# Layer 0 of a four-layer cross-attention stack: values summed by head, spread over the array by class, with one output matmul a tile, in place of values folded with the output weights

## The chip, the cores and the metric

One core of one Trainium2 chip runs the whole kernel in one launch. The metric is the device time in microseconds (us) of one execution. A profile of one execution gives the time of every instruction on TensorE (PE), VectorE (DVE), ScalarE (ACT), GpSimd (POOL) and the DMA queues that SyncE (SP) issues. All data are float32 but for the masks (bfloat16). A float32 matmul shows as two records (a weight load and a matmul each twice), so 8 matmuls are 16 records.

## What is computed

Four attention layers follow each other on 8 sequences of 256 positions and 128 features, with a context of 64 positions and 64 features. The change is in layer 0, cut here to what matters:

```python
q = (x @ Wq.T)            # B=8, L=256, 16 heads of 8 features
k = (ctx @ Wk.T) + pos    # M=64 context positions
v = (ctx @ Wv.T)
attn = softmax(q @ k.T * 8 ** -0.5)            # per head, over the 64 positions
attn_out = attn @ v                            # 16 heads of 8 features: 128
memory_output = attn_out @ Wo.T
gate = sigmoid(silu(concat(x, mean(ctx)) @ gate_w1.T + b1) @ gate_w2.T + b2)
enhanced = layernorm(x + gate * memory_output)
x = where(entropy(softmax(x @ ent_w)) > 1, enhanced, x)
```

Layer 1 is an attention with one head, layer 2 six blocks of self-attention (masked, 16 heads of 64), cross-attention and feed-forward, layer 3 an attention whose softmax runs over the positions of the sequence. These are the same before and after.

## The kernel before

The work stands in a plan. `at(tick, phase, fn)` enters a step; at the end (lines 1251 to 1261) the steps are written out tick by tick and, within a tick, by phase, and each engine takes its instructions in exactly that order. The engines wait for each other by semaphores alone. PSUM is a pool of four tiles of two banks each (line 37): every product takes the next free one, and its first matmul waits until the last reader of the tile before it there is done. SBUF tiles rotate within a tag in the same way.

Layer 0 handles sequence b in ticks from T = 2b on (`plan_l0`, lines 662 to 740), in two tiles of 128 queries. Tile number n (0 to 15) is thus handled in ticks n to n + 3, and several tiles are in flight at once. The steps of one tile (`plan_weights_64`, lines 314 to 399):

- `scores`, tick n, phase 1: 16 matmuls (L328) into two banks. Partition class a (32 partitions each) holds the heads 4a to 4a+3, the columns hold query block, head of the class and context position.
- `lower`, phase 2: ScalarE copies the scores to SBUF (L357), VectorE takes the maximum of each head (L359), which starts when the copy has ended, and GpSimd subtracts it (L360).
- `exps`, phase 8: ScalarE takes the exponential in place (L366).
- `divide`, tick n + 1, phase 2.4: VectorE sums and takes the reciprocal (L370, L371), GpSimd multiplies (L372).
- `turn`, tick n + 2, phase 2.5: VectorE turns 32x32 blocks (L380), so that the partitions hold the class and the context position.
- `sums`, tick n + 3, phase 3: 8 matmuls of 128x128 by 128 (L388) add up weights times folded values into the output of 128 queries by 128 features, and `take` (L687 on VectorE) applies the gate and adds the residual.

Beside these a sequence has, in even ticks, `queries` (L667, evacuated at L671, phase 3.3 of tick T - 2), `spread_keys` (GpSimd, L675), `make_values` (phase 3.2 of tick T + 2: 16 matmuls at L303, one copy of 128x1024 on ScalarE at L309), `moments` (phase 6 of T + 4: VectorE L262/L263 and four small steps on GpSimd, L265 to L696), in odd ticks `normal` (phase 2.95 of T + 5: ScalarE, L701 and L706) and `scaled` (phase 4.8: two transposes L713, evacuated at L715), and in even ticks `mix` (phase 4.7 of T + 6: two transposes L721, taken by L724). Layer 1 (`plan_l1`) follows for each sequence from tick 2b + 7 on, at phases 4.2 to 4.5: L749 and L780 are its transposes, L757, L761 and L789 its matmuls, L766, L778 and L794 its steps on VectorE, L751, L772 and L782 those on ScalarE. From tick 11 on the first projections of layer 2 (L861, L867, L880, L808 to L843) stand in the same ticks; its first scores (L898) come in tick 17.

The fold: since attn_out @ Wo.T is linear, the value weights and output weights of each head can be multiplied beforehand. `spread_outputs` (L523, GpSimd) spreads the output weights by head, `turn_values` (L530, L533) turns the value weights, and `fold_l0` (L545, four matmuls of 512 columns, and four copies on ScalarE, L552) makes WVO, 128 features for each head. `values_of` (lines 295 to 312) then multiplies the context with it. These steps stand in ticks -1, 1 and 2, among the steps that compute the gates (`gate_inputs` L490, `gate_hidden` L501 and L502, which takes turns between ScalarE and VectorE, `gates` L508), the logits (L447, after the selectors of L444) and the masks (L624, stored to DRAM by L631 and fetched later).

Two pairs of large tiles, `room` (line 85), hold the small weights of the start; the tag "eTc" that two of them come from is taken again by layer 2's weights from tick 17 on.

Of the kernel before, what the change touches and what calls it, by code (L numbers as in the profile page):

```python
# [16 lines left out]
P = 128  # L17
# [10 lines left out]
def tile_xattn_stack(ctx: ExitStack, tc: tile.TileContext, io, out: bass.AP):  # L28
# [22 lines left out]
    def tp_tile():  # L51
        return one_bank("tp")

    def mm_tile():
        return one_bank("mm")
# [134 lines left out]
        nc.vector.tensor_copy(hmask8[rows], hmask[rows, 8 * r : 8 * r + 8])  # L190


    W = {}

    def load_sa(l):
# [83 lines left out]
    def at(tick, phase, fn):  # L279
        plan.setdefault(tick, []).append((phase, fn))  # L280
# [33 lines left out]
    def plan_weights_64(tick, qt, qT, keys, values, mask, take):  # L314

        tl = {}

        def scores():  # L320
            sc = two_banks("sc").rearrange("p (q x) -> p q x", q=4)
            if mask is None:
                for i in range(4):
                    for a in range(4):
                        q = (i + 2 * (a // 2)) % 4
                        rows = slice(64 * (a // 2), 64 * (a // 2) + 64)
                        qb = 4 * qt + q
                        nc.tensor.matmul(  # L328
                            sc[32 * a : 32 * a + 32, q, :],
                            lhsT=qT()[rows, qb * 32 : (qb + 1) * 32],  # L330
                            rhs=keys()[rows, 4 * (a % 2) : 4 * (a % 2) + 4, :].rearrange(
                                "p h k -> p (h k)"
                            ),
                            start=True, stop=True,
                        )
                tl["sc"] = sc.rearrange("p q x -> p (q x)")
                return
            for q in range(4):
                qb = 4 * qt + q
                for a in range(4):  # L340
                    nc.tensor.matmul(  # L341
                        sc[32 * a : 32 * a + 32, q, :],
                        lhsT=qT()[:, qb * 32 : (qb + 1) * 32],
                        rhs=keys()[:, a].rearrange("p h k -> p (h k)"),
                        start=True, stop=False,
                    )
                for a in range(4):
                    nc.tensor.matmul(
                        sc[32 * a : 32 * a + 32, q, :], lhsT=ones0, rhs=mask,
                        start=False, stop=True,  # L350
                    )
            tl["sc"] = sc.rearrange("p q x -> p (q x)")

        def lower():
            sc = tl.pop("sc")
            e = big("e", shape=(P, 16, M))
            nc.scalar.copy(e.rearrange("p h k -> p (h k)"), sc)  # L357
            m = sm([P, 16], "m16")
            nc.vector.tensor_reduce(m, sc.rearrange("p (h k) -> p h k", k=M), AX.X, ALU.max)  # L359
            nc.gpsimd.tensor_tensor(  # L360
                e, e, m.unsqueeze(2).to_broadcast([P, 16, M]), ALU.subtract
            )
            tl["e"] = e

        def exps():
            nc.scalar.activation(tl["e"], tl["e"], AF.Exp)  # L366

        def divide():
            r = sm([P, 16], "r16")
            nc.vector.tensor_reduce(r, tl["e"], AX.X, ALU.add)  # L370
            nc.vector.reciprocal(r, r)  # L371
            nc.gpsimd.tensor_tensor(  # L372
                tl["e"], tl["e"], r.unsqueeze(2).to_broadcast([P, 16, M]), ALU.mult
            )

        def turn():
            e = tl.pop("e").rearrange("p (q h) (k x) -> p (h k) q x", q=4, x=32)
            eT = big("k" if mask is None else "o", shape=(P, 8, 4, 32))
            for i in range(2):
                nc.vector.transpose(eT[:, 4 * i : 4 * i + 4], e[:, 4 * i : 4 * i + 4])  # L380
            tl["eT"] = eT

        def sums():
            ps = mm_tile()
            eT, vw = tl.pop("eT"), values()
            for s in range(8):
                g, r, k = s // 4, s // 2 % 2, s % 2
                nc.tensor.matmul(  # L388
                    ps[:, :D], lhsT=eT[:, s].rearrange("p q x -> p (q x)"),
                    rhs=vw[:, r, k, g, :], start=(s == 0), stop=(s == 7),  # L390
                )
            take(ps)

        at(tick, 1, scores)
        at(tick, 2, lower)
        at(tick, 8, exps)
        at(tick + 1, 2.4, divide)
        at(tick + 2, 2.5, turn)
        at(tick + 3, 3.0, sums)


    S0 = {}
# [115 lines left out]
        nc.vector.tensor_copy(flag, ps[:, :B])  # L518
        nc.vector.tensor_scalar(nflag, flag, -1.0, 1.0, ALU.mult, ALU.add)

    def spread_outputs():
        S0["wobd"] = place("first", H * D).rearrange("p (h d) -> p h d", h=H)
        nc.gpsimd.tensor_tensor(  # L523
            S0["wobd"], w0o.unsqueeze(1).to_broadcast([P, H, D]),
            hmask.unsqueeze(2).to_broadcast([P, H, D]), ALU.mult,
        )

    def turn_values():
        tps = tp_tile()
        nc.tensor.transpose(tps[:, :DM], w0v, ident[:DM, :DM])  # L530
        wv2 = S0["wv2"] = place("second", P)
        for r in range(2):
            nc.scalar.copy(wv2[:, r * DM : (r + 1) * DM], tps[:, :DM])  # L533

    def fold_l0():


        wobd, wv2 = S0["wobd"], S0["wv2"]
        S0["WVO"] = sb([P, HC, D], "WVO", 1, heap)
        wvo = S0["WVO"].rearrange("p (g a) d -> p a g d", g=2)  # L540
        for half in range(2):
            ps = two_banks("mm")
            for i in range(2):
                a = 2 * half + i
                nc.tensor.matmul(  # L545
                    ps[:, i * 512 : (i + 1) * 512], lhsT=wv2,
                    rhs=wobd[:, 4 * a : 4 * a + 4].rearrange("p h d -> p (h d)"),
                    start=True, stop=True,
                )
            for r in range(2):  # L550
                rows = slice(r * DM, (r + 1) * DM)
                nc.scalar.copy(  # L552
                    wvo[rows, 2 * half : 2 * half + 2],
                    ps[rows].rearrange("p (a g r d) -> p a g r d", a=2, g=2, r=2)[:, :, :, r, :],
                )

    def fold_l1():

# [77 lines left out]
    def plan_start():  # L636
        at(-4, 0, lambda: turn_x(0))
        at(-4, 1, keys_l0)
        at(-4, 2, pool_context)
        at(-1, 0, spread_outputs)  # L640
        for c in range(1, 4):
            at(0, 3.1 + 0.1 * c, lambda c=c: turn_x(c))
        at(0, 3.6, gate_context)
        at(1, 3.0, gate_inputs)
        at(1, 3.1, gate_hidden)
        at(1, 3.2, turn_values)
        for i in range(4):
            at(1, 8.5, lambda i=i: mask(i))
        at(1, 8.6, store_masks)
        at(2, 3.1, fold_l0)  # L650
        at(2, 3.4, gates)
        at(2, 3.6, logits)
        at(3, 4, entropy)
# [8 lines left out]
    def plan_l0(b, T):  # L662
# [15 lines left out]
            )  # L678

        def make_values():  # L680
            st["VW"] = values_of(b, S0["WVO"])

        def add(qt, ps):
            if qt == 0:
# [57 lines left out]
    def plan_l1(b, T):  # L742
# [34 lines left out]
        def turn():  # L777
            nc.vector.reciprocal(st["r"], st["r"])  # L778
            tps = tp_tile()
            nc.tensor.transpose(tps[:, :P], st.pop("e"), ident)  # L780
            st["eT"] = sb([P, P], "o0")
            nc.scalar.copy(st["eT"], tps[:, :P])  # L782

        def values():
# [534 lines left out]
```

## Time and profile before

| what | us |
|---|---|
| median of 3 runs | 2443.6 (2442.93 to 2445.48) |
| the profiled execution | 2442.87 |
| its span, from the first to the last instruction | 2441.1 |
| PE busy, share of the span | 2349.7, 96% |
| DVE busy | 1839.3, 75% |
| ACT busy | 1718.1, 70% |
| POOL busy | 1450.2, 59% |
| PE busy from 0 to 44 us (the start, ticks 0 to 2) | 33.33 of 44 |
| PE busy from 44 to 145 us (ticks 3 to 16) | 93.28 of 101 |
| PE busy from 145 to 172 us (ticks 17 to 19) | 22.39 of 27 |
| PE busy from 172 us to the end | 2200.70 of 2269 |

Busy time of PE counts from the start of a matmul to its modelled end, so a PE that is busy is not PE at its peak. In the page's slices each digit is the busy share of a fortieth of the span (61 us) in tenths. A row of the timeline or of the groups is: start, length, engine, line, operation, output<-inputs, the form, how many, and in brackets the idle time before it with what ended it. For matmuls the form begins with the part of the array that is used: 128*32 is 128 rows and 32 columns. The chain of waits lists start, length and what: it follows the work that ended last back through what released it; cut to a window it begins with the last work of that window. A row of a table by windows has the stretch, its length, the busy time (and number) on PE, PE's weight loads, DVE, ACT and POOL, then the granted TensorE clock as a share of full speed, the DMA share and GB/s.

### The profile page before, as it was taken

How to read it: one execution, taken by the hardware profiler on the slowest of the kernel's cores; microseconds unless marked ns; L12 is line 12 of the kernel's file. 1: busy time of each engine (PE TensorE's matmuls, PEld its weight loads, DVE VectorE, ACT ScalarE, POOL GpSimd, SP SyncE). 2: the span in 40 equal slices, each digit the busy share in tenths (PEclk: the TensorE clock that was granted, in tenths of full speed). 3: DMA queues.
4: the chain of work that ended last, by engine and by line, in shares of the span. 5: the costliest groups of instructions: out<-in, count | busy, mean ns of one | idle time of the engine just before them, and what ended most of it. 6: DMA issues, size and time to landing. Idle time of an engine off the chain costs nothing.

```text
span 2441.1 us, 99984 instructions
## 1 busy us (share of the span) xinstructions
PE 2349.7 (96%) x42411; PEld 1742.3 (71%) x42411; DVE 1839.3 (75%) x5988; ACT 1718.1 (70%) x4528; POOL 1450.2 (59%) x2483
## 2 busy tenths in 40 slices
PE   8999999999999999999999999999999999999986
PEld 4667777777777677777777777777777777777764
DVE  5778887677887667887767887667888667888664
ACT  5577777677777667777667777667777667778642
POOL 4845557754556755556855556755556765555763
PEclk9999999999999999999999999999999999999998
DMA  6000022000022001022001022001012000010000
GB/s 177 2 11 14 23 75 57 2 12 21 20 72 64 2 3 30 20 72 64 2 3 30 20 63 64 11 3 30 20 55 72 12 2 26 24 53 5 2 3 16
DMA packets 102833, 76.88 MB, mean 31 GB/s; under 512 B 8113, under 2 KB 96881, under 8 KB 102386
## 3 DMA queue, kind: packets, MB, share of 16 engines
q1 hardware_dynamic: 101794, 70.16, 10.4%
q8 instruction: 334, 5.47, 0.9%
q14 instruction: 113, 0.93, 0.1%
q10 hardware_dynamic: 592, 0.33, 0.1%
HBM read 62.07 MB, written 8.39 MB: 29 GB/s over the span
## 4 chain that ended last, share of the span: by engine, by line
PE 77%; DVE 8%; ACT 7%; POOL 5%; issue 2%; DMA 0%; SPq 0%; POOLq 0%; DVEq 0%; ACTq 0%
PE mm L861 14%; PE sc L898 14%; PE mm L953 13%; PE mm L971 7%; PE mm L880 7%; PE mm L388 5%; PE sc L341 4%; PE mm L1120 3%; PE mm L1137 2%; DVE m L359 2%; ACT e L357 2%; POOL e L360 2%; PE mm L1079 2%; PE tp L841 1%; PE mm L303 1%
## 5 line engine op out<-in xcount | busy, mean ns | idle before, releaser
L927 POOL TENSOR_SCALAR e<-e,rs 128x256 f32<-128x256 f32 x1536 | 703.0, 478 | 673.3 <-DVE rs L925 664.0
L917 ACT ACTIVATE e<-e,mn 128x256 f32<-128x256 f32 x1536 | 758.2, 495 | 133.8 <-DVE mn L912 129.5
L912 DVE CUSTOM_DVE_ANT_0 e<-sc,nm 128x256 f32<-128x256 f32 x1536 | 542.4, 419 | 107.7 <-PE sc L898 106.2
L937 DVE STREAM_TRANSPOSE eTc<-e 128x512 f32<-128x512 f32 x768 | 517.3, 695 | 62.5 <-POOL e L927 61.2
L898 PE MATMUL sc<-k,q 64*32 64x256 f32 x12288 | 377.7, 380 | 1.9 <-ACT v L286 1.0
L953 PE MATMUL mm<-eTc,v 32*64 32x256 f32 x12288 | 363.9, 377 | 5.7 <-ACT AT L1054 3.3
L953 PEld LDWEIGHTS mm<-eTc,v 32*64 32x64 f32 x12288 | 277.3, 131 | 88.7 <-issue 22.7
L359 DVE TENSOR_REDUCE m<-sc 128x16 f32<-128x1024 f32 x112 | 136.7, 1221 | 269.2 <-ACT e L357 269.2
L360 POOL TENSOR_TENSOR e<-e,m 128x1024 f32<-128x1024 f32 x112 | 213.1, 1902 | 209.8 <-DVE m L359 209.8
L898 PEld LDWEIGHTS sc<-k,q 64*32 64x32 f32 x12288 | 221.3, 106 | 122.2 <-issue 48.9
L917 ACT ACTIVATION_READ_ACCUMULATOR e<-e,mn 128x1 f32 x1536 | 287.1, 187 | 0.0
L341 PE MATMUL sc<-q,tT 128*32 128x256 f32 x3072 | 222.0, 388 | 3.0 <-DVE t L1104 2.3
L372 POOL TENSOR_TENSOR e<-e,r 128x1024 f32<-128x1024 f32 x112 | 213.0, 1902 | 2.9 <-DVE r L371 2.9
L388 PE MATMUL mm<-v,o 128*128 128x128 f32 x1536 | 202.2, 287 | 0.0
L388 PEld LDWEIGHTS mm<-v,o 128*128 128x128 f32 x1536 | 188.9, 201 | 16.1 <-issue 8.7
L861 PE MATMUL mm<-tT,w_sk 128*128 128x256 f32 x768 | 189.1, 389 | 0.0
L971 PEld LDWEIGHTS mm<-w_sow,o 128*128 128x128 f32 x1536 | 175.1, 192 | 17.0 <-issue 12.3
L880 PE MATMUL mm<-w_sv,tT 128*32 128x256 f32 x3072 | 185.7, 382 | 0.0
L286 ACT COPY v<-mm 128x1024 f32<-128x1024 f32 x96 | 97.2, 1012 | 124.3 <-PE mm L880 123.7
L971 PE MATMUL mm<-w_sow,o 128*128 128x128 f32 x1536 | 183.6, 278 | 0.8 <-ACT WVO L1052 0.8
L861 PE MATMUL mm<-tT,w_sq 128*128 128x256 f32 x768 | 173.6, 379 | 0.0
L861 PEld LDWEIGHTS mm<-tT,w_sk 128*128 128x128 f32 x768 | 138.1, 190 | 44.1 <-issue 29.2
(212 smaller groups left out, 3544.5 us busy)
## 6 DMA issues: line engine op xcount, KB each, us to landing
nm<-mask_d SPq DMA_DIRECT2D x192, 128.0 KB
wd<-o SPq DMA_DIRECT2D x48, 128.0 KB
w_sk<-in_L_sa_kv_dram SPq DMA_DIRECT2D x6, 512.0 KB
w_sv<-in_L_sa_kv_dram SPq DMA_DIRECT2D x24, 128.0 KB
w_sq<-in_L_sa_q_dram SPq DMA_DIRECT2D x6, 512.0 KB
w_sow<-in_L_sa_ow_dram SPq DMA_DIRECT2D x6, 512.0 KB
w_ckv<-in_L_ca_kv_dram SPq DMA_DIRECT2D x12, 256.0 KB
w_cq<-in_L_ca_q_dram SPq DMA_DIRECT2D x6, 512.0 KB
```

The source lines that it names most:

```text
L341: nc.tensor.matmul(sc[32 * a : 32 * a + 32, q, :], lhsT=qT()[:, qb * 32 : (qb + 1) * 32], rhs=keys()[:, a].rearrange("p h k -> p (h k)"), ...
L360: nc.gpsimd.tensor_tensor(e, e, m.unsqueeze(2).to_broadcast([P, 16, M]), ALU.subtract)
L388: nc.tensor.matmul(ps[:, :D], lhsT=eT[:, s].rearrange("p q x -> p (q x)"), rhs=vw[:, r, k, g, :], start=(s == 0), stop=(s == 7),)
L861: nc.tensor.matmul(ps[:, i * S : (i + 1) * S], lhsT=w[:, c * P : (c + 1) * P], rhs=st["tT"], start=True, stop=True,)
L880: nc.tensor.matmul(ps[32 * a : 32 * a + 32, i, :], lhsT=st["tT"][:, kb * 32 : (kb + 1) * 32], rhs=sv[:, a].rearrange("p g x -> p (g x)"), ...
L898: nc.tensor.matmul(sc[32 * a : 32 * a + 32, r, j, :], lhsT=st["q"][g][rows, a, qb * 32 : (qb + 1) * 32], rhs=st["k"][g][rows, a, :], start ...
L912: nc.vector.tensor_tensor_reduce(e[:, i, :], sc4[:, i, :], st["nm"][:, 2 * jj + i % 2, :], -1.0, 3.0 * BIG, ALU.add, ALU.min, mn[:, i : i ...
L917: nc.scalar.activation(e[:, i, :], e[:, i, :], AF.Exp, scale=-1.0, bias=mn[:, i : i + 1], accum_out=rs[:, i : i + 1],)
L927: nc.gpsimd.tensor_scalar(e[:, i, :], e[:, i, :], rs[:, i : i + 1], 1.0, ALU.mult, ALU.mult)
L937: nc.vector.transpose(eT[:, r, :, 2 * jj : 2 * jj + 2, :], e[:, 2 * r : 2 * r + 2, :].rearrange("p j (k x) -> p k j x", x=32),)
L953: nc.tensor.matmul(ops[a // 2][r * HD : (r + 1) * HD, a % 2, :S], lhsT=st["v"][kb // 4][rows, kb % 4, (2 * g + r) * HD : (2 * g + r + 1) * ...
L971: nc.tensor.matmul(st["ps"][:, j * D : (j + 1) * D], lhsT=st["oT"][c // 4][:, c % 4, j * P : (j + 1) * P], rhs=sow[:, c, :], start=(c == 0 ...
```

## The change

Layer 0 no longer folds the output weights into the values. The values of a sequence are 8 features for each head: 8 matmuls of 64x32 weights by 32 columns, and one multiply on VectorE spreads them by class, with a mask `cmask` that leaves in partition class a only the 8 columns of the head that belongs to it (the array of 128 rows thus holds four heads at a time, and each sums only its own class). The sums of a tile are 8 matmuls of 128x32 weights by 128 queries, four column groups of the array in turn, two in each sum; they give the attention output with features on partitions. ScalarE copies it to SBUF (oT), and one matmul with the output weights, whose rows are put in the same order of features by `turn_outputs`, gives what `take` needs, at phase 4.6 of the same tick. In layer 0 the exponentials move from phase 8 of tick n to phase 2.05 of tick n + 1, behind the copy of the next tile's scores. `spread_outputs`, `turn_values` and `fold_l0` go. The tag "o0", which layer 1's L782 uses too, has three tiles in place of two. Layer 2's cross-attention shares `plan_weights_64` and keeps its steps.

```diff
@@ -188,6 +188,18 @@
     for r in range(2):
         rows = slice(64 * r, 64 * r + 64)
         nc.vector.tensor_copy(hmask8[rows], hmask[rows, 8 * r : 8 * r + 8])
+
+
+    cmask = const.tile([P, 4], F32, tag="cmask", name="cmask")
+    nc.gpsimd.memset(cmask, 1.0)
+    nc.gpsimd.affine_select(
+        out=cmask, in_=cmask, compare_op=ALU.is_ge, fill=0.0, base=0,
+        pattern=[[-32, 4]], channel_multiplier=1,
+    )
+    nc.gpsimd.affine_select(
+        out=cmask, in_=cmask, compare_op=ALU.is_ge, fill=0.0, base=31,
+        pattern=[[32, 4]], channel_multiplier=-1,
+    )
 
 
     W = {}
@@ -380,6 +392,26 @@
                 nc.vector.transpose(eT[:, 4 * i : 4 * i + 4], e[:, 4 * i : 4 * i + 4])
             tl["eT"] = eT
 
+        def sums_by_head():
+            ps = mm_tile()
+            eT, vw = tl.pop("eT"), values()
+            for k in range(2):
+                for j in range(4):
+                    nc.tensor.matmul(
+                        ps[32 * j : 32 * j + 32, :P], lhsT=vw[:, 4 * k + j, :],
+                        rhs=eT[:, 2 * j + k].rearrange("p q x -> p (q x)"),
+                        start=(k == 0), stop=(k == 1),
+                    )
+            tl["oT"] = sb([P, P], "o0", 3)
+            nc.scalar.copy(tl["oT"], ps[:, :P])
+
+        def outputs():
+            ps = mm_tile()
+            nc.tensor.matmul(
+                ps[:, :D], lhsT=tl.pop("oT"), rhs=S0["wo"], start=True, stop=True
+            )
+            take(ps)
+
         def sums():
             ps = mm_tile()
             eT, vw = tl.pop("eT"), values()
@@ -393,10 +425,15 @@
 
         at(tick, 1, scores)
         at(tick, 2, lower)
-        at(tick, 8, exps)
         at(tick + 1, 2.4, divide)
         at(tick + 2, 2.5, turn)
-        at(tick + 3, 3.0, sums)
+        if mask is None:
+            at(tick + 1, 2.05, exps)
+            at(tick + 3, 3.0, sums_by_head)
+            at(tick + 3, 4.6, outputs)
+        else:
+            at(tick, 8, exps)
+            at(tick + 3, 3.0, sums)
 
 
     S0 = {}
@@ -518,41 +555,17 @@
         nc.vector.tensor_copy(flag, ps[:, :B])
         nc.vector.tensor_scalar(nflag, flag, -1.0, 1.0, ALU.mult, ALU.add)
 
-    def spread_outputs():
-        S0["wobd"] = place("first", H * D).rearrange("p (h d) -> p h d", h=H)
-        nc.gpsimd.tensor_tensor(
-            S0["wobd"], w0o.unsqueeze(1).to_broadcast([P, H, D]),
-            hmask.unsqueeze(2).to_broadcast([P, H, D]), ALU.mult,
+    def turn_outputs():
+
+        perm = place("first", P)
+        nc.gpsimd.tensor_copy(
+            perm.rearrange("p (j a f) -> p j a f", j=4, a=4),
+            ident.rearrange("p (a j f) -> p j a f", j=4, a=4),
         )
-
-    def turn_values():
-        tps = tp_tile()
-        nc.tensor.transpose(tps[:, :DM], w0v, ident[:DM, :DM])
-        wv2 = S0["wv2"] = place("second", P)
-        for r in range(2):
-            nc.scalar.copy(wv2[:, r * DM : (r + 1) * DM], tps[:, :DM])
-
-    def fold_l0():
-
-
-        wobd, wv2 = S0["wobd"], S0["wv2"]
-        S0["WVO"] = sb([P, HC, D], "WVO", 1, heap)
-        wvo = S0["WVO"].rearrange("p (g a) d -> p a g d", g=2)
-        for half in range(2):
-            ps = two_banks("mm")
-            for i in range(2):
-                a = 2 * half + i
-                nc.tensor.matmul(
-                    ps[:, i * 512 : (i + 1) * 512], lhsT=wv2,
-                    rhs=wobd[:, 4 * a : 4 * a + 4].rearrange("p h d -> p (h d)"),
-                    start=True, stop=True,
-                )
-            for r in range(2):
-                rows = slice(r * DM, (r + 1) * DM)
-                nc.scalar.copy(
-                    wvo[rows, 2 * half : 2 * half + 2],
-                    ps[rows].rearrange("p (a g r d) -> p a g r d", a=2, g=2, r=2)[:, :, :, r, :],
-                )
+        ps = mm_tile()
+        nc.tensor.matmul(ps[:, :D], lhsT=perm, rhs=w0o, start=True, stop=True)
+        S0["wo"] = place("first", D)
+        nc.vector.tensor_copy(S0["wo"], ps[:, :D])
 
     def fold_l1():
 
@@ -637,17 +650,15 @@
         at(-4, 0, lambda: turn_x(0))
         at(-4, 1, keys_l0)
         at(-4, 2, pool_context)
-        at(-1, 0, spread_outputs)
         for c in range(1, 4):
             at(0, 3.1 + 0.1 * c, lambda c=c: turn_x(c))
         at(0, 3.6, gate_context)
         at(1, 3.0, gate_inputs)
         at(1, 3.1, gate_hidden)
-        at(1, 3.2, turn_values)
+        at(1, 3.2, turn_outputs)
         for i in range(4):
             at(1, 8.5, lambda i=i: mask(i))
         at(1, 8.6, store_masks)
-        at(2, 3.1, fold_l0)
         at(2, 3.4, gates)
         at(2, 3.6, logits)
         at(3, 4, entropy)
@@ -678,7 +689,24 @@
             )
 
         def make_values():
-            st["VW"] = values_of(b, S0["WVO"])
+
+
+            ps = mm_tile()[:, : 2 * 32].rearrange("p (k x) -> p k x", k=2)
+            for k in range(2):
+                for a in range(4):
+                    nc.tensor.matmul(
+                        ps[32 * a : 32 * a + 32, k, :],
+                        lhsT=ctx2[:DM, b, 32 * k : 32 * k + 32],
+                        rhs=w0v[:, 32 * a : 32 * a + 32], start=True, stop=True,
+                    )
+            st["VW"] = big("v")[:, :256].rearrange("p (s x) -> p s x", x=32)
+            nc.vector.tensor_tensor(
+                st["VW"].rearrange("p s (a f) -> p s a f", a=4),
+                ps.rearrange("p k (j f) -> p (k j) f", j=4).unsqueeze(2).to_broadcast(
+                    [P, 8, 4, 8]
+                ),
+                cmask.unsqueeze(1).unsqueeze(3).to_broadcast([P, 8, 4, 8]), ALU.mult,
+            )
 
         def add(qt, ps):
             if qt == 0:
@@ -778,7 +806,7 @@
             nc.vector.reciprocal(st["r"], st["r"])
             tps = tp_tile()
             nc.tensor.transpose(tps[:, :P], st.pop("e"), ident)
-            st["eT"] = sb([P, P], "o0")
+            st["eT"] = sb([P, P], "o0", 3)
             nc.scalar.copy(st["eT"], tps[:, :P])
 
         def values():
```

## The prediction

> **What bounds the kernel now.** I read the page's 40 slices first, then the chain of work that ended last, cut to the first 175 us, then the timeline of single ticks. The change touches layer 0 alone, and by the waits of the built program nothing after tick 19 differs, so only the stretch from 0 to about 172 us can move; what is gained there is handed on, since from there on TensorE binds.
>
> ```profile
> PE   8999999999999999999999999999999999999986
> DVE  5778887677887667887767887667888667888664
> ACT  5577777677777667777667777667777667778642
> ```
>
> By these tenths TensorE is full from the second slice (61 us) on. Inside layer 0 that misleads: the chain runs through all engines. The start, start and length in us:
>
> ```profile
> 28.59 0.21 ACT eTc L533 x2
> 28.84 5.24 PE mm L545 x8
> 34.11 0.59 ACT WVO L552
> 34.74 1.67 PE mm L303 x24
> 36.40 0.63 PE mm L667 x2
> 37.03 3.66 PE mm L508 x32
> 40.69 3.56 PE mm L447 x16
> ```
>
> The fold (L533, L545, L552) stands ahead of the gates (L508) and logits (L447) on TensorE, and tick 3's scores come only behind them, at 44.17. An even tick, scores at 78.47, next scores at 85.03:
>
> ```profile
> 78.47 1.97 PE sc L328 x32
> 80.46 1.02 ACT e L357
> 81.51 1.22 DVE m L359
> 82.73 1.14 DVE r L370
> 83.89 0.25 DVE r L371
> 84.14 1.16 DVE k L380 x2
> 85.30 0.23 DVE y L687
> ```
>
> This is a ring: scores, copy, maximum, sum, reciprocal, turn. It stands 6.85 us after its start when TensorE's own work has just let the next scores go. An odd tick, scores at 97.66, next at 102.82, ScalarE in the timeline:
>
> ```profile
> 101.25 0.88 ACT L701 ACTIVATE y<-y,nm,rstd 128x128 f32<-128x128 f32 x2 [0.35 <-POOL nm L696]
> 102.03 0.49 ACT L706 ACTIVATE tb<-t,nflag 128x256 f32<-128x256 f32 x1
> 102.43 0.24 ACT L782 COPY o<-tp 128x128 f32<-128x128 f32 x1
> ```
>
> Here nothing that TensorE needs for its next scores stands behind the copies to come on ScalarE; the scores' slot is free.
>
> **The change, part by part.**
>
> *TensorE's work.* Per tile the 8 matmuls of L388 (1.98 us in the chain) become 8 of 128x32 weights by 128 columns, and one of 128x128. The shape is not in the trace. Nearest rows: L880, 128x32 by 256 columns, 32 records in 1.86 us, 58 ns each; L898, 64x32, 64 records in 1.89, 30 ns each. So 16 records at 30 to 58 ns are 0.5 to 0.9 us; I take 0.55. The output matmul is an eighth of L388, 0.25. Per sequence the values go from 1.02 (L303) to 16 records, 0.5. If TensorE bound the stage this were 16x1.2 + 8x0.5, 23 us; the rings say that most of it is not on the path.
>
> *The start.* spread_outputs (GpSimd, 3.61 us at 9.62) goes, but GpSimd is idle until 15.77: nothing. In tick 1 the exponentials now stand behind copy 1, so the first sum on VectorE moves from 20.92 to about 20.3, and the sigmoid chain L501/L502 ends 0.3 earlier, at 28.75. The perm copy on GpSimd stands behind two L360/L372 of 1.90 and lands near 24.9; TensorE waits for it (3.2 us behind L490), tick 2's scores go from 21.8 to 25.2, and ScalarE is in its sigmoids until 28.25 anyway: nothing. Without the fold the gates run from 29.5 to 33.2, but the logits' selectors are now late: on VectorE behind the wo copy (0.2), four masks (2.45), maximum, sum, reciprocal, turn (3.8), the new values multiply (0.37) and the copies (0.6), so the logits begin at 35.75 instead of 40.69 and tick 3's scores at 39.3: **4.9 us ahead**. Tick 3 ends with the output matmul behind ScalarE's copy 3, exponentials and oT; scores of tick 4 at 43.85, before 49.85: 6.0 ahead.
>
> *The new waits.* The values' product moves from ScalarE (L309, 1.01) to VectorE, behind the turn. L608, a tensor_tensor out of PSUM, is 1.23 for 1024 columns; L687 0.23 for 128; for 256 I take 0.37 (ends 0.23 and 1.23). It frees the bank that the mix of the same tick (L721) takes, and TensorE's next scores queue behind that. An even tick is therefore 6.85 + 0.37 = 7.2; from tick 10 on, where VectorE's L1 adds (L794, 0.52) follow and free the scores' bank, 7.75. In an odd tick the output matmul waits for oT, on ScalarE behind the copy (1.0), the moved exponentials (1.0), normal (0.78) and kept (0.40), and the transposes of scaled and the next scores queue behind it: 1.99 to the copy + 0.97 + 1.0 + 0.78 + 0.40 + 0.24 + 0.8 (matmul, two transposes, semaphores) = 6.15, before 5.2. What the moved exponentials take away (ScalarE's wait for GpSimd, 0.77 before 91.59) is thus paid back.
>
> *The sum by ticks*, start of scores before and as I work it out: tick 5 57.18 and 52.6; 6 63.89 and 59.1; 7 70.39 and 64.8; 8 78.47 and 71.55 (6.9 ahead); then 7.2 and 6.15: tick 10 90.24 and 84.9; 7.75 and 6.15: tick 12 102.82 and 98.8, 4.0 ahead. So the rings cost 1.4 per pair of ticks. In ticks 12 to 16 projections of layer 2 fill TensorE and the saved matmuls count again: tick 12 with L832's 1.9 on VectorE 10.05 (before 9.85), tick 13 9.4 (10.3), 14 7.75 (8.5), 15 and 16 13.7 (13.85). Layer 2's first scores come at 139.7, before 145.29. In ticks 17 and 18 ScalarE binds (eight exponentials of 0.495, then oT and three copies): 0.2 lost each, some TensorE time won. **About 5.6 us ahead** at 165, and kept, since I left out some semaphore steps of 0.02 to 0.08. The SP queue and its DMAs are unchanged; the masks stored at 33.92 come at nearly the same time, and layer 2's weights are there by 60.
>
> The profiled execution took 2442.87 (span 2441.1 and 1.8 around it): 2442.87 - 5.6 = 2437.3. The median is 0.7 above it: **2438.0**.
>
> [...]
>
> The clock: from 168.50 to 171.90 TensorE ran two transposes only, and the granted clock was 0.50 in the next 3.4 us.
>
> ```profile
> 168.50:171.90 3.40, 0.66 (x2) 0.28 (x2) 2.37 (x7) 3.40 (x11) 2.33 (x5) 1.00 0.00 0
> 171.90:175.30 3.40, 3.25 (x64) 1.55 (x64) 2.17 (x12) 1.64 (x7) 2.94 (x7) 0.50 0.00 0
> ```
>
> In the new odd ticks TensorE has, from 2.6 to 6.15 after the scores' start, only transposes and one matmul: 3.5 us. [...]
>
> **Rivals.**
> 1. *TensorE is the bound after all*: the rings are looser than I read (another bank order, a shorter product), and the saving counts. For it: 93.3 of 101 us busy from 44 to 145. Against: the chain above. The start's 4.9 and two fifths of the 23 (the ticks that layer 2 fills and every second one before): 2443.6 - 14 = 2430.
> 2. *The rings eat the start's gain*: if the product takes 1.23, seven even ticks lose 0.86 more each, 6 us: 2443.6, no change. Against: 256 columns, not 1024.
> 3. *Slower*: the half clock in the odd ticks. Scores at half clock took 3.53 (at 172.05) instead of 1.89, 1.65 more on the path each time. Four drops use the gain up; in all six odd ticks it is 10 - 5.6 = 4.4 over before: 2448. For it: the gap of 3.5. Against: the output matmul stands inside it, and idle stretches of 1.9 (at 112.15) dropped nothing.
> 4. *It doesn't do what it says*: the output matmul, one for eight, is there in the built program; nothing to give.
>
> **Chances.** My case 0.72: 2433 to 2441, of which 0.50 is more than 4.9 us (0.2%, about what a measurement of this kernel can tell from no change) below 2443.6 and 0.22 less. Rival 1 0.10, rival 2 0.10, rival 3 0.08. Faster 0.60, same 0.32, slower 0.08. For 8 in 10 the range goes from 2432, which is 2 short of rival 1, to 2445, which takes in rival 2 and the highest run of before within 0.5.
>
> **What would show it.** Right: tick 3's scores near 39, tick 8's near 71.5, then even ticks of 7.2 to 7.8 whose next scores wait for VectorE's product or L1 add, odd ticks of about 6.1 whose output matmul waits for ScalarE's oT; layer 2's first scores 4 to 7 us earlier; everything later shifted by that. Wrong: odd ticks that stay at 5.2 (rival 1), a product near 1.2 us (rival 2), a granted clock of 0.5 inside 45 to 145 us (rival 3), or logits that start before 34 us, which would make the start worth more.

## The result, and the profile after

The changed kernel takes 2443.26 us (median of 20 runs), the kernel before 2444.52 (20 runs taken with them). The ratio is 0.9994, 95% interval 0.9985 to 1.0003: no change that can be measured, where 5.6 us (0.23%) less was forecast. One of the 20 runs of the changed kernel took 8038 us, a slow one: the ratio is taken without it, and the median of the other 19 is 2443.17. The profiled execution took 2442.09 (span 2440.4). Layer 2's first scores, the mark of the end of layer 0 in the prediction, come at 149.56, not at 139.7, and later than before (145.29).

The page of the changed kernel, the slices of TensorE and of the granted clock, and under them the clock's slices in the kernel before:

```profile
PE   7789999999999999999999999999999999999996
PEclk8899999999999999999999999999999999999998
```

```profile
PEclk9999999999999999999999999999999999999998
```

The first two slices (0 to 122 us) have lost TensorE work, as intended. But PEclk shows 8 in the same two slices, where it was 9. The table by windows puts the two kernels side by side from 57 to 145 us, about ticks 5 to 16; the figure behind POOL's is the granted clock. The kernel before, then the changed one:

```profile
57.00:145.00 88.00, 81.13 (x975) 58.85 (x975) 65.77 (x138) 52.46 (x93) 64.27 (x63) 1.00 0.01 2
```

```profile
57.00:145.00 88.00, 70.63 (x861) 42.96 (x857) 61.20 (x126) 46.77 (x97) 59.04 (x60) 0.86 0.01 1
```

TensorE is busy 10.5 us less, and its granted clock is 0.86 on average instead of 1.00. In the records of these two profiles the granted clock is 1.0 or 0.5, and up to 153 us a stretch at 0.5 is 3.41 us long or two, three or four times that (6.83, 10.24 and 13.65). Ahead of layer 2's first scores it is 0.5 for 38.3 us in the changed kernel, and for 3.4 us before. (The record of the clock begins at 14.9 us before and at 12.2 in the changed kernel; tick 0's scores, which start ahead of that, take 3.64 and 3.21 us instead of 1.9.)

What half clock does to a tick shows in the chain of waits of the changed kernel, an even tick and an odd one (the scores' start, length and line):

```profile
74.25 1.91 PE sc L340 x32
...
79.78 1.24 DVE k L392 x2
81.02 0.32 DVE v L703
...
81.38 3.68 PE sc L340 x32
...
86.00 1.06 ACT e L378
87.05 0.77 ACT y L729 x2
87.82 0.40 ACT tb L734
88.22 0.16 ACT o L406
...
88.42 0.80 PE mm L410 x2
89.22 0.43 PE tp L741 x2
89.64 3.61 PE sc L340 x32
```

The even tick, 74.25 to 81.38, is the ring as predicted, VectorE's product (L703) its last link. In the odd tick the chain also runs as predicted: copy, exponentials (L378), normal (L729), kept (L734), the copy oT (L406), the output matmul (L410), two transposes. But its scores take 3.68 instead of 1.91, the output matmul 0.80 instead of 0.49 (at 61.09, at full clock) and the transposes 0.43 instead of 0.22: 8.2 us instead of 6.15.

The windows of the clock around it, TensorE's busy time first after the length, the granted clock behind POOL's:

```profile
77.08:80.49 3.41, 2.09 (x14) 1.45 (x13) 3.23 (x5) 1.51 (x4) 2.32 (x3) 1.00 0.00 0
80.49:83.90 3.41, 2.52 (x24) 1.16 (x28) 2.42 (x9) 0.70 (x4) 2.54 (x3) 0.50 0.01 2
83.90:87.32 3.42, 2.96 (x31) 1.29 (x23) 1.19 (x2) 2.23 (x3) 1.61 (x4) 0.50 0.00 0
87.32:90.73 3.41, 2.31 (x16) 1.41 (x20) 2.86 (x7) 2.05 (x7) 3.29 (x2) 0.50 0.00 0
90.73:94.15 3.42, 3.42 (x40) 1.37 (x32) 0.00 (x0) 0.87 (x1) 1.15 (x2) 0.50 0.00 0
```

From 77.08 to 80.49 TensorE is busy 2.09 of 3.41 us, and the next window is granted 0.50. It stays so for four windows, in three of which TensorE again stands idle for 0.45 to 1.1 us, and it ends behind the one that is filled (from 94.15 on it is 1.00 again). The start has the same. These are the gates and the logits in the timeline:

```profile
28.69 6.46 PE L545 MATMUL mm<-L_w2T,k 64*128 64x1 f32 x32
35.08 5.80 PE L484 MATMUL mm<-eTc,eTc 128*8 128x256 f32 x16
```

Before, they took 3.66 and 3.56. There the clock fell too, from 28.54 to 31.95, but the fold's matmuls, which the change takes away, stood in that window and filled it (3.11 of 3.41 us busy), and the clock was 1.00 again when the gates came. Tick 3's scores come at 40.81 instead of the 39.3 of the prediction.

### The profile page after: what moved, and what is told of

Its sections match the earlier page's. It is cut to its first block, busy times and chain, and to the rows that moved or that the text cites. A ratio compares the mean times of both kernels' runs of the same rounds, so it can differ in the third digit from the quotient of the medians.

```text
span 2440.4 us, 99807 instructions
## 1 busy us (share of the span) xinstructions
PE 2333.8 (96%) x42308; PEld 1719.6 (70%) x42308; DVE 1842.6 (76%) x5997; ACT 1710.8 (70%) x4530; POOL 1447.2 (59%) x2486
## 2 busy tenths in 40 slices
DMA packets 102832, 76.87 MB, mean 31 GB/s; under 512 B 8113, under 2 KB 96881, under 8 KB 102386
## 4 chain that ended last, share of the span: by engine, by line
PE 75%; DVE 9%; ACT 8%; POOL 5%; issue 2%; DMA 1%; SPq 0%; POOLq 0%; ACTq 0%; DVEq 0%
PE mm L889 14%; PE sc L926 14%; PE mm L981 13%; PE mm L999 7%; PE mm L908 7%; PE sc L353 4%; PE mm L420 4%; PE mm L1165 2%; PE mm L1148 2%; DVE m L371 2%; ACT e L369 2%; POOL e L372 2%; PE mm L1107 1%; PE tp L869 1%; ACT e L945 1%
```

## The experiments

**The theory**: the rings are as worked out, and TensorE with less to do falls to half clock in layer 0, which takes the gain back. **Rivals**: the new waits (oT behind ScalarE's copies, VectorE's product) are dearer than worked out; the moved exponentials; the start.

All runs in one table. Half clock is the time granted 0.50, ahead of 57 us and from there to layer 2's first scores (give or take 0.1 us); "ring time" is from tick 5's scores to layer 2's first scores, in the profile, of which each kernel has one. Ratios are to the kernel before, run beside each (its medians there are 2444.14 to 2445.28).

| kernel | half clock, us | tick 5 | ring time | layer 2 | median, us (runs) | ratio, 95% |
|---|---|---|---|---|---|---|
| before | 3.4 + 0 | 57.18 | 88.1 | 145.29 | 2444.52 (20) | |
| predicted | | 52.6 | 87.1 | 139.7 | 2438.0 | 0.9977 |
| changed | 13.6 + 24.7 | 54.88 | 94.7 | 149.56 | 2443.26 (20) | 0.9994, 0.9985 to 1.0003 |
| again | 19.2 + 14.8 | 57.09 | 91.8 | 148.90 | 2442.1 (1) | |
| exps_back | 17.0 + 20.4 | 56.45 | 92.5 | 148.90 | 2443.08 (12) | 0.9989, 0.9977 to 1.0001 |
| warm_ticks | 19.7 + 0.8 | 58.05 | 87.0 | 145.01 | 2438.06 (12) | 0.9977, 0.9964 to 0.9990 |
| warm_one | 13.6 + 11.1 | 56.85 | 89.8 | 146.60 | 2438.60 (11) | 0.9977, 0.9967 to 0.9987 |
| warm_turns | 13.6 + 3.4 | 55.71 | 88.4 | 144.09 | 2439.83 (11) | 0.9980, 0.9968 to 0.9993 |
| warm_all | 6.8 + 4.6 | 60.09 | 90.7 | 150.83 | 2447.51 (12) | 1.0009, 0.9996 to 1.0023 |
| rings | 20.0 + 14.1 | 54.82 | 90.2 | 145.00 | 2437.64 (12) | 0.9972, 0.9963 to 0.9981 |
| start | 18.4 + 12.2 | 57.41 | 89.1 | 146.55 | 2442.26 (12) | 0.9998, 0.9988 to 1.0007 |
| rings_start | 16.5 + 17.5 | 53.62 | 91.5 | 145.10 | 2434.12 (7) | 0.9964, 0.9946 to 0.9981 |
| rings_warm | 13.6 + 0 | 55.88 | 84.5 | 140.34 | 2433.90 (5) | 0.9960, 0.9948 to 0.9973 |
| rings_start_warm | 13.6 + 0 | 54.04 | 84.7 | 138.76 | 2434.09 (9) | 0.9969, 0.9955 to 0.9982 |
| warm_start | 3.4 + 4.3 | 55.16 | 86.1 | 141.30 | 2432.50 (7) | 0.9961, 0.9947 to 0.9974 |

**again**: the changed kernel, one more execution.

> The changed kernel as it is, one more execution. Clock theory: in layer 0 the half clock comes from the thinner work itself, so it comes back: 25 to 50 us at 0.50 before 152 us (41 in the first profile, 3.4 in the kernel before), at other places perhaps, and layer 2's first scores at 146 to 152 (149.56 in the first profile). Rival, a chance of the first execution: under 10 us at 0.50, and layer 2's first scores at 139 to 142, as predicted. Rival, the rings alone: first scores at 149 to 150 whatever the clock shows.

34 us at half clock, at other places than in the first profile, and layer 2's first scores at 148.90. It is no chance of one execution. The clock of all runs says the same: the mean granted clock of the whole kernel is 0.9817 over 19 runs of the changed kernel (0.980 to 0.983), and 0.986 to 0.987 over the 24 to 29 runs of the kernel before in each of the later batches (0.983 to 0.990). As time at half clock, (1 - clock) x 2 x span, this is 89 us against 66 to 68: the change adds some 22 us of it. The same mean over the runs of the other kernels goes along with their profiles: 0.9814 in exps_back and 0.9815 in start, which leave the ticks thin, 0.9843 in warm_one, 0.9849 in warm_turns and 0.9854 in warm_ticks, which fill them.

**exps_back**: the exponentials where they were.

```diff
-            at(tick + 1, 2.05, exps)
+            at(tick, 8, exps)
```

> The changed kernel with the exponentials put back where the kernel before has them, at the end of their own tick behind the normal and kept steps, instead of behind the next tick's scores copy. If the moved exponentials are what lengthens odd ticks (they stand ahead of the per-head sums' copy on ScalarE), layer 2's first scores come 3 to 5 us earlier, at 145 or 146, and the time is 2438 to 2440. Clock theory: nothing of the kind; within 1.5 us of the changed kernel by the clock's places alone, and with ScalarE's wait for GpSimd back (0.77 a pair of ticks) rather later: 149 to 154.

The same as the changed kernel, in the first scores (148.90) and in time. The moved exponentials are not what eats the gain.

**warm_ticks**: work for TensorE that nothing needs, in the gap ahead of each output matmul. It goes into the second bank of the output's tile, which is unused, so no tile is added and no wait of another engine.

```diff
-            ps = mm_tile()
+            both = two_banks("mm")
+            ps = both[:, :512]
+            for _ in range(2 if 4 <= tick + 3 <= 13 else 0):
+                nc.tensor.matmul(
+                    both[:, 512:768], lhsT=S0["wo"], rhs=xT[:, 512:768], start=True, stop=True
+                )
             nc.tensor.matmul(
                 ps[:, :D], lhsT=tl.pop("oT"), rhs=S0["wo"], start=True, stop=True
```

(Here and in the edits below, the number of added matmuls is written into the loop; the kernels hand it to `outputs` as an argument where the step is entered.)

> The changed kernel with two extra matmuls (128x128 by 256 columns, results not used) ahead of each output matmul in ticks 4 to 13 only, where TensorE waits in those ticks; the start and the ticks from 14 on are left as they are. Clock theory: no or one window at 0.50 between 57 and 145 us; from tick 5's scores to layer 2's first scores 87 to 89 us (94.7 and 91.8 in two profiles of the changed kernel, 88.1 in the kernel before), so layer 2's first scores at 143 to 145 and a time of 2437 to 2440. Ring theory: 91 to 95 us for that stretch whatever the clock, and a time of 2442 to 2446.

This is what the clock theory expects, and the ring theory does not: 20 added matmuls shorten the ring time by 5 to 8 us and the kernel by 4 to 5 (0.17% by the ratios, 5.2 us by the medians). Two windows of warm_ticks, an even tick's and an odd tick's, at the place of the table above:

```profile
78.34:81.76 3.42, 2.74 (x58) 1.40 (x50) 1.21 (x2) 2.09 (x5) 1.43 (x2) 1.00 0.02 5
85.17:88.58 3.41, 2.70 (x51) 1.41 (x43) 1.90 (x7) 2.29 (x6) 2.38 (x6) 1.00 0.00 0
```

TensorE is busy 2.7 of 3.4 us in both, and the clock stays at 1.00. With the clock held, the ring time is 86.96 us; the prediction's own sum was 87.1.

**warm_one**: one matmul instead of two.

```diff
-            for _ in range(2 if 4 <= tick + 3 <= 13 else 0):
+            for _ in range(1 if 4 <= tick + 3 <= 13 else 0):
```

> As warm_ticks, but one extra matmul a tile instead of two (0.5 us of TensorE work a tick instead of 1.0). If the granted clock depends on how much of each 3.4 us TensorE is busy: fewer half-clock windows than the changed kernel's 15 to 25 us between 57 us and layer 2's first scores, but more than warm_ticks' 0.8; about 5 to 10 us, and 88 to 91 us from tick 5's scores to layer 2's. If any work at all in the gap is enough: as warm_ticks, 87.

In between: 11.1 us at half clock, 89.8. So in this kernel not any work was enough; by this one profile (11.1 us between 0.8 and 24.7), and by the mean clock of the runs (0.9843 between 0.9854 and 0.9817), it goes by how much. In time warm_one can't be told from warm_ticks (2438.60 and 2438.06).

**warm_turns**: transposes in the place of the two matmuls.

```diff
-            for _ in range(2 if 4 <= tick + 3 <= 13 else 0):
-                nc.tensor.matmul(
-                    both[:, 512:768], lhsT=S0["wo"], rhs=xT[:, 512:768], start=True, stop=True
-                )
+            for _ in range(5 if 4 <= tick + 3 <= 13 else 0):
+                nc.tensor.transpose(both[:, 512:640], xT[:, 512:640], ident)
```

> As warm_ticks, but the extra work ahead of each output matmul is five 128x128 transposes (about 1 us, as long as the two matmuls). If TensorE's busy time of any kind keeps the clock, or if warm_ticks gains by something else than the clock (by the order of waits, say): as warm_ticks, 87 us from tick 5's scores to layer 2's and a time near 2438. If transposes do not count as busy: half-clock windows as in the changed kernel, 15 us or more, 91 to 95 us, and 2442 to 2446.

The five take 0.72 to 0.76 us, less than I had meant, and still do nearly what the matmuls do: one window at half clock instead of four to seven. (A transpose shows as one record, a float32 matmul as two, so these five are five records.) A window with one set of them in it, in warm_turns, behind which the clock is 1.00 as well:

```profile
84.25:87.66 3.41, 2.00 (x28) 1.21 (x24) 2.12 (x2) 3.16 (x6) 3.12 (x6) 1.00 0.00 0
```

Over ticks 4 to 13 as a whole these float32 transposes went with less half clock (3.4 us instead of 24.7 and 14.8 in the changed kernel). This single window doesn't show it: with 2.00 us busy it is as thin as the one of 2.09 us behind which the changed kernel's clock fell, and windows of this size went both ways (half clock behind three of nine, last section).

**warm_all**: two or, in odd ticks, three such matmuls in every tick of layer 0, and five and six ahead of the gates and the logits.

```diff
+            for _ in range(3 if tick % 2 == 0 else 2):
...
+        for _ in range(5):
+            nc.tensor.matmul(
+                both[:, 512:768], lhsT=S0["wo"], rhs=xT[:, 512:768], start=True, stop=True
+            )
         for n in range(NT):
...
+        for _ in range(6):
+            nc.tensor.matmul(
+                both[:, 512:768], lhsT=S0["wo"], rhs=xT[:, 512:768], start=True, stop=True
+            )
         for b in range(B):
             nc.tensor.matmul(
                 lg_ps[:B, :S], lhsT=esel[:, b, :], rhs=xT[:, b * S : (b + 1) * S],
```

> The changed kernel with extra matmuls (128x128 by 256 columns, results not used) where TensorE waits anyway: five ahead of the gates, six ahead of the logits, two or three ahead of each output matmul of layer 0, in the unused second bank of a tile that is there already. Clock theory: the granted clock stays at 1.0 from 26 to 150 us but for a window or two, scores take 1.9 us everywhere, and layer 2's first scores come at 139 to 143, 7 to 10 us before the changed kernel's 149.56; the time falls by as much, to 2432 to 2436. Ring theory (the new waits for the per-head sums' copy and the values' product eat the gain): 149 or later, since the added matmuls can only delay, and the time is 2443 or more.

A miss. The clock is up from 61 to 149 us, and the even and odd ticks are 7.2 and 6.25. But at the start the added matmuls stand ahead of work that was ready and run at half clock for a part themselves (3.58 us for the five and 4.54 for the six, where two take 1.03 at 71.31; tick 3's scores at 44.78 instead of 40.81), and in ticks 15 and 16, which layer 2's projections fill, they are on the path (15.5 for the last two ticks instead of 13.8). Extra work paid here only where TensorE waits (2438.06 in warm_ticks, 2447.51 in this one). This run alone would have spoken for the ring theory.

**rings**: what the new waits cost. The copy oT goes directly behind the scores' copy, the values' product ahead of the row sum.

```diff
-            at(tick + 3, 3.0, sums_by_head)
+            at(tick + 3, 2.04, sums_by_head)
...
-        at(T + 2, 3.2, make_values)
+        at(T + 2, 2.06, make_values)
```

> The changed kernel with the copy of the per-head sums on ScalarE and the values' product on VectorE moved ahead: the copy directly behind the scores' copy and ahead of the exponentials, the product ahead of the row sum and turn. Ring theory: odd ticks at full clock shorten from 6.2-6.5 to about 5.5, even ones from 7.2 to 6.9 or not at all; six pairs give 4 to 6 us, layer 2's first scores at 143 to 146, time 2437 to 2440. Clock theory: single ticks at full clock shorten by that, but the half clock stays (20 us or more at 0.50 before 150), so that layer 2's first scores come at 145 to 149 and the time falls by 1 to 4 us only.

In the timeline of rings, tick 8 (scores at 74.94 to 76.87), the copy oT now starts 1.0 us behind the scores' end, and the output matmul of the even tick has nothing to wait for:

```profile
77.84 0.27 ACT L406 COPY o<-mm 128x128 f32<-128x128 f32 x1
...
79.11 0.41 DVE L703 TENSOR_TENSOR v<-mm,cmask 128x256 f32<-128x256 f32 x1
...
79.53 0.44 PE L410 MATMUL mm<-eTc,o 128*128 128x128 f32 x2
...
80.12 1.93 PE L340 MATMUL sc<-q,xn 64*32 64x256 f32 x32
```

That even tick is 5.18 long instead of 7.20. The ring time is 90.2 with 14 us at half clock still in it, and the kernel gains 5.6 us on the changed one. So both theories hold a part. With the clock held in both, warm_ticks and **rings_warm** (rings with the two matmuls) tell the waits' share alone: 87.0 and 84.5, 2.5 us, by one profile each.

> The rings kernel with the two extra matmuls a tile in ticks 4 to 13, without the start's new order. Rings and clock together: 84 to 86 us from tick 5's scores to layer 2's (90.2 in rings, 87.0 in warm_ticks, 84.7 in rings_start_warm); time 2434 to 2437. If the start's order is what makes rings_start_warm fast: 87 or more, and 2437 or later.

**start**: the selectors in tick 0, the logits ahead of the gates, L1's key bias loaded ahead of the masks.

```diff
+    b1k = column("L1_bk")
     mask_v = io["mask_BxSxS_ik0"].rearrange("b (h p) k -> p b h k", p=P)
...
-    b1k = column("L1_bk")
...
+        at(0, 2.3, selectors)
...
-        at(2, 3.6, logits)
+        at(2, 3.25, logits)
```

> The changed kernel with the start put in another order: the eight selector copies in tick 0, the logits ahead of tick 2's queries and of the gates (in the gap in which TensorE waits for the sigmoid chain, 26.1 to 28.1), and L1's key bias loaded ahead of the masks instead of behind them. Clock and queue theory: the gates and logits no longer run at half clock (6.5 and 5.8 us there), tick 3's scores come at 34 to 37 instead of 40.8; the wait for the bias at 50.4 is gone, tick 5's scores come at 46 to 50 instead of 54.9 to 57.1. What is gained there stays if the rings of the later ticks bind: layer 2's first scores at 141 to 144, time 2434 to 2438. Rival: the start is not what bounds the end of layer 0 (masks, weights or the clock of ticks 5 to 13 take it back), and the first scores come at 147 or later, time within 2 us of the changed kernel.

The rival holds. Tick 3's scores come at 37.94, 2.9 earlier, but tick 5's at 57.41, later than in the changed kernel, and the time is unchanged. **rings_start** has the edits of rings and of start:

> The earlier copy and product of the rings kernel together with the start of the start kernel. If the two add up (rings: about 4.5 us at layer 2's first scores against the changed kernel; start: 5 to 8): first scores at 136 to 141, time 2428 to 2434. If they share one limit (a DMA, the masks, or the half clock, which a start with less TensorE work makes likelier): no better than the better of the two.

Layer 2's first scores at 145.10, as in rings (145.00); the two don't add up there. The medians differ by 3.5, but the intervals lie one within the other.

**rings_start_warm**: the edits of rings, start and warm_ticks.

> The rings and start kernels together, with the two extra matmuls a tile in ticks 4 to 13. Clock theory: what is left of the half clock between 57 and 145 us in rings_start (15 to 25 us at 0.50, 0.5 us of path each 1 us of scores) is 2 to 5 us of path, so layer 2's first scores come 2 to 5 us ahead of rings_start's. Rival: TensorE is no longer waiting in these ticks and the extra matmuls (1 us a tile) are on the path: 2 to 8 us later than rings_start.

The clock theory's side, with more than was expected: layer 2's first scores 6.3 us earlier than in rings_start. In time the two are alike all the same (2434.1 both), so rings_start's one profile (2444.52, the longest of its seven runs) shows more half clock than most of its runs had (a mean clock of 0.979, where the other six have 0.982 to 0.985).

**warm_start**: rings_start_warm with added matmuls in the gaps of ticks 1, 2, 3 and 4 as well, each time in the unused bank of a tile that is there.

```diff
         both = two_banks("mm")
         ps = both[:, :512]
+        for _ in range(4):
+            nc.tensor.matmul(
+                both[:, 512:768], lhsT=ident, rhs=xT[:, 512:768], start=True, stop=True
+            )
         nc.tensor.matmul(ps[:, :D], lhsT=perm, rhs=w0o, start=True, stop=True)
...
+            for _ in range(2 if tick + 3 == 4 else 0):
...
+            for _ in range(2 if T == 6 else 0):
...
-            for _ in range(2 if 4 <= tick + 3 <= 13 else 0):
+            for _ in range(2 if 3 <= tick + 3 <= 13 else 0):
```

> The rings_start_warm kernel with the extra matmuls in the start's gaps too: four ahead of the permuted output weights' matmul (TensorE waits there 2.9 us), four behind the gates, two ahead of tick 4's sums and two ahead of its queries, and in tick 3. Clock theory: of the 13.6 us at half clock before 57 us most go, tick 5's scores come at 49 to 52 instead of 54.1, and layer 2's first scores at 134 to 137; time 2430 to 2433. Rival: the start is bound by the chain through VectorE and ScalarE and by activation-table loads, whatever the clock: tick 5's scores at 53 or later, nothing gained.

Another miss: of 13.6 us at half clock ahead of 57 us 3.4 are left, and tick 5's scores still come at 55.16. In its timeline VectorE works without a gap from 45.80 to 56.4, through tick 4's sum and turn, the entropy's steps, the bias and the next maximum. The changed kernel has the same chain: TensorE stands idle for 2.81 us ahead of 51.20, until VectorE's bias step is done. So tick 4 is bound by VectorE in large part. How much the clock adds, warm_start doesn't tell, since its added matmuls also cost: tick 3's scores come at 39.03, behind the 36.47 of rings_start_warm.

**What beats both**: rings_warm, 2433.90, 0.9960 (0.9948 to 0.9973), 11 us less than the kernel before. The start's edits add nothing to it that these runs can tell.

## Why the prediction was right or wrong

The figures of the prediction stand in brackets.

**Right, the unit costs.** The eight sums take 0.64 in the timeline, 0.57 of them until the next product starts (0.55), VectorE's product 0.31 to 0.42 (0.37), the values 0.33 a sequence (0.5). The output matmul takes 0.22 to 0.50 of the chain of waits at full clock (0.25), in the odd ticks 0.49.

**Right, the rings.** At full clock the even tick is 7.20 (predicted 7.2), from tick 10 on 7.71 (7.75); the odd one 6.22 in the second profile and 5.97 in warm_ticks (6.15); ticks 12, 13 and 14 take 9.80, 9.45 and 7.71 in warm_ticks (10.05, 9.4, 7.75), 15 and 16 together 13.5 (13.7). Rival 1 is out, TensorE doesn't bind; rival 2 too, the product isn't 1.23. That new waits take the place of TensorE's saving was right as well; what they cost, 2.5 us, is what rings_warm gets back.

**Wrong, the step that left the clock out of the sum.** The sum by ticks prices every tick at full clock and puts half clock at nothing. Rival 3 had the mechanism and got 0.08. I set a window's idle time against 3.4 us and let one matmul inside the gap count as cover: "the output matmul stands inside it, and idle stretches of 1.9 (at 112.15) dropped nothing". The window of 77.08 to 80.49 answers that: it holds most of the queries' matmul, four small products, an output matmul and two transposes, 2.09 us busy, and the clock fell. The stretch ahead of 112.15 of the kernel before was no safe case either. Its window was thinner still, and the clock happened to stay:

```profile
110.46:113.87 3.41, 1.64 (x26) 0.96 (x30) 3.34 (x11) 1.03 (x5) 1.04 (x1) 1.00 0.00 0
```

I also priced half clock per scores (1.65) and as four to six drops, all in odd ticks; it comes in even ones too, and in the start.

The price that the runs give: over the seven profiles with the changed rings and the start's or ticks' clock varied (changed, again, exps_back, start, warm_one, warm_turns, warm_ticks) the ring time is 86.7 + 0.30 x (us at half clock), correlation 0.97 (with warm_all, whose added matmuls are on the path, 0.90); over the five with the earlier copies 84.5 + 0.39 x. The changed kernel's 24.7 us cost it 7.4 by that, of the 7.6 that its ring time is over the forecast.

**In the range by luck.** 2443.26 lies inside the range of 2432 to 2445, but outside the 2433 to 2441 of my case. The upper end was put there for rival 2, the dear product, which the runs rule out. A gain and a loss that I had priced apart, one of them at nothing, came out nearly equal.

**Wrong, the start, by 2.3 to 5.5 us.** Tick 3's scores 1.5 late, since gates and logits ran at half clock; tick 5's at 54.88 to 58.05 in profiles of the same start, not 52.6. That half clock isn't all of it: warm_start took most of it away and gained nothing at tick 5. VectorE's chain of tick 4 binds in large part; my step of 8.75 for that tick is short of the 9.4 to 11 that it takes in these profiles.

**No term for a change of form.** In the kernel before 0.41 us without a weight load stand ahead of L388 (80.33) and L667 (83.34), 0.13 ahead of L303 (82.32, behind the last load of L388) and 0.17 ahead of the scores at 85.03. The sum has no term for these stretches, and the ticks at full clock above came out within 0.2 of it without one.

**A window need not be empty.** The drop of the kernel before at 28.54 came behind a window without a TensorE record (25.12 to 28.54). In the windows ahead of the changed kernel's six drops up to 149 us TensorE did work, 1.07 to 2.09 us: 1.39 from 25.88 to 29.29, 2.09 from 77.08 to 80.49. The window of the prediction's row, 168.50 to 171.90, with two transposes, was thinner still (0.66 us). It doesn't say that transposes go for nothing: in warm_turns five a tile left 3.4 us at half clock, where the changed kernel has 24.7 and 14.8.

**"About 5.6 us ahead and kept."** Kept, yes, but blurred: from layer 2's first scores to the end the 14 profiles take 2288.8 to 2297.7 us, and this goes with the time at half clock in it (46 to 68 us; 0.40 us for each, correlation 0.90), which falls at other places in each execution. It doesn't go with when layer 2 starts (correlation 0.16).

**Open.** The kernel before has one profile. By it layer 0 ends 4.3 us ahead of the changed kernel's, and by the medians the changed kernel is 1.3 us ahead. The rest of the two programs is the same; in that profile it took 2295.9, in the changed kernel's two 2290.8 and 2291.5. The half clock there (60.8, 55.1 and 54.3 us) accounts, at 0.40 each, for some 2.5 of the 4.7. Whether the remainder is chance, or the first profile of before shows a quicker layer 0 than it mostly has, no run here shows. All runs together hint at the second. Over the 80 later runs of the kernel before, the time goes with the mean clock (correlation -0.93, 0.39 us for each us at half clock), and at the same mean clock of 0.983 the kernel before takes 2448.7 to 2454.6 (5 runs), the changed one 2438.4 to 2441.4 (4 runs), some 12 us less. The half clock lies at other places in the two, so this is no measure of the change alone. It suggests that without the added half clock the change would have gained what was forecast, or more.

## What to carry to other kernels

Before counting TensorE work taken away as a gain, read its busy time window by window (3.41 us in these traces), not by its longest idle gap: in this kernel, thinning it until windows fell to 2.09 us and less brought half clock behind six of them, 38.3 us of it ahead of layer 2's first scores, on all that stood on the path there. Where a stage is bound by other engines, matmuls or transposes that nobody needs, put exactly where TensorE waits, held the clock (0.8 and 3.4 us at half clock instead of 24.7) and paid here (2443.3 to 2438.1 and 2439.8); put ahead of ready work they cost (2447.5). And a step that now waits for another engine's copy is to be put behind the earliest copy that it needs, since everything queued ahead of it becomes its latency (2.5 us here).

## What the runs showed of the hardware

The counts are over the profiles of the kernel before and of the changed one, in windows of 3.41 us that begin where the clock's stretches do, from the first record of the clock to 161 us. (The ends of matmuls are modelled, so the busy times are rough.)

- Behind windows at full clock: with up to 1.39 us of matmul records four of four were followed by half clock (0.00 in the kernel before; 1.39, 1.07 and 1.36 in the changed one), with 1.64 to 2.09 us three of nine (1.82, 2.09 and 1.97, all in the changed kernel; 1.64, 2.01 and 2.04 in the kernel before and 1.67, 1.81 and 2.00 in the changed one were not), with 2.27 us or more none of 61. What decided between 1.64 and 2.09 us, no run here shows.
- Behind windows at half clock: with 2.31 to 2.96 us busy four of four were followed by half clock again, with 3.11 and 3.17 us none of two, and of seven that were filled two, both with the gates' matmuls in them.
- Two windows that records cover were followed by half clock all the same. In the changed kernel's windows at half clock that the gates fill (29.29 to 32.70, and most of 32.70 to 36.12), 64x1 matmuls of one column each, the clock stayed at 0.50; behind the window of the logits (36.12 to 39.53), 128 rows by 8 columns of the array and 256 columns moving, it was 1.00. From the window ahead of the drop on:

```profile
25.88:29.29 3.41, 1.39 (x24) 0.98 (x18) 2.34 (x7) 2.78 (x4) 0.00 (x0) 1.00 0.23 44
29.29:32.70 3.41, 3.41 (x18) 3.41 (x18) 3.41 (x5) 2.95 (x4) 0.94 (x1) 0.50 0.75 200
32.70:36.12 3.42, 3.42 (x15) 2.74 (x16) 2.48 (x14) 0.92 (x2) 3.42 (x3) 0.50 1.06 341
36.12:39.53 3.41, 3.41 (x9) 1.10 (x8) 0.00 (x0) 0.64 (x1) 0.40 (x1) 0.50 1.16 345
39.53:42.94 3.41, 3.41 (x50) 1.55 (x52) 1.28 (x4) 0.68 (x3) 0.00 (x0) 1.00 0.94 289
```
